# A conditioned transformer block on one core: where the transposed maxima's parts and their spreading stand among scores and values, and which queue carries the inverses

## The chip, the cores and the metric

The kernel runs on one core of a Trainium2 chip. The metric is device time in microseconds, the median of several runs. One further execution was taken with the hardware profiler; all spans, waits and clocks below are from that execution.

## What is computed

One block on x of shape (4, 1024, 512), in float32 throughout: a conditioned RMS norm, attention with 16 heads of 32, a second conditioned RMS norm and a SwiGLU feed-forward of width 2048, with the residual added twice.

```
norm(x)  = g(t) * x * rsqrt(mean(x*x) + 1e-6) + b(t)
a        = x + softmax(q k^T / sqrt(32)) v @ Wo.T     # q, k, v from norm1(x)
block(x) = a + (silu(n @ gate.T) * (n @ hid.T)) @ out.T   # n = norm2(a)
result   = x + block(x)
```

## The kernel before

The tokens are cut into 8 blocks of 512. Scores stand transposed, keys on the partitions, so one unit of score work r covers 256 keys, 4 heads and 256 queries: a tile `raw` of 128 x 2048. Four such units (256 keys each, 1024 in all) make one j, that is one group of heads for 256 queries. The main loop runs over slots g; slot g computes the scores of unit g, and g % 4 (`kind`) says which quarter of its j it is. Work on other units lies in the same slot: adding the shift and the exponential to unit g - 5 (`r_x`), multiplying unit g - 6 by the values (`r_v`).

For each j the softmax needs the maximum over all keys, which lie on partitions and in the four units. `running_max` (L290, L293) folds units elementwise into `rmax`; `max_T` (L299) transposes it on TensorE into a tile `mt` that shares the score banks `sc`; `parts` (L305 to L310) reduces on VectorE and splits the negated maximum into three bfloat16 parts in `split`; `parts_T` transposes them on TensorE (`pt`, L315) and copies them on ScalarE to `mT` (L317); `spread` multiplies them by a selecting matrix on TensorE (`sp`, L325), which puts the shift of two heads on all partitions, and copies that on ScalarE to `shift` (L326); it is called for heads 0 and 1 and for heads 2 and 3. `shifted` (VectorE, L330) adds `shift` to `raw`, `exponential` (ScalarE, L335) follows, and `weighted` (TensorE, `av`, L345) multiplies by the values. `keep` (ScalarE, L285) copies the scores from their bank to `raw`; the score tile `sc` has one buffer, so the next scores (L278) wait for it.

The denominators: `accumulate` adds the exponentials by a DMA from GpSimd's queue (L359), `fold_sum` (L367) folds them on VectorE, `sums` (TensorE, L377) sums over the keys, `sums_out` (ScalarE, `total`, L382) copies. The sums then go through DRAM to be inverted in a compact form: `compact` (L146), `take` (L152), `invert` (VectorE, L157), `put` (L162), and `spread_inverse` (L168), which reads each row to 32 partitions in four DMAs, the tile `rec`. All these DMAs are issued from ScalarE's queue. `normalize` (VectorE, L402) uses `rec` in the kind-2 slot after. The second norm's inverse roots `inv` take the same way (`norm_root`, `norm_compact`, `take`, `invert`, `put`, `norm_spread`), with slots given by `after(g0 + ...)` (end of the slot) and `between(g0 + ...)` (towards its end), where g0 = 32 (n + 1) for block n; then follow `norm_scale` (VectorE, L179), `norm_mod` (ScalarE, L182) and `token_sums` (VectorE, L465 to L471).

From slot 60 on (`FS`) the feed-forward of block n runs beside the attention of later blocks: one of 16 hidden tiles p for two slots, even and odd. It is computed with seven products of half size (a Strassen-like form): in the even slot `pair_26` (`pa`), `copy_156` (ScalarE, L516, to `pb`) and the contraction of an earlier tile (`filler`, `pc`, taken by VectorE in L554); in the odd slot `pair_7` (`pb`), `sub_5` (VectorE, L523), `pair_3` (`pa`), `gate_tanh` (ScalarE, L533), `pair_15` of the next tile (`pa`), `take_5` (ScalarE, L497), `gate` (VectorE, L538), `add_15` (VectorE, L501), `pair_4` (`pb`, which needs `sub_5`) and `hidden` (VectorE, L541). Before slot 60 the projections of keys, queries and values stand there instead (`chain`, with an `evict` in the slot or, for `late`, at the head of the next one).

Two banks of PSUM (tag `w` of pool `ps`) are shared by `pa`, `pc`, `pt`, `sp`, `sum`, `pm` (the norm's mean) and the projections: while `pa` holds one, the chain pc, pt, sp, sp, next pa goes through the other, each waiting until an engine has emptied it.

The order of instructions on TensorE, VectorE, ScalarE and GpSimd is the order of the calls in the code (a manual schedule). SyncE's queue, which carries the weights (`fw`: L477, L478, L480, L481; `ow`: L545; `wo`: L410), the loads of `kq` (L257, L258), `v` (L264) and `res` (L406), and the stores of keys and values (`st`, `sv`: L236, L249), is ordered by the scheduler. DMAs from SyncE and ScalarE share eight completion semaphores in turn, so that a DMA also waits until the previous one on its semaphore has landed.

Of the kernel before, what the change touches and what calls it, by code (L numbers as in the profile page):

```python
# [24 lines left out]
def tile_cond_transformer_block(  # L25
# [138 lines left out]
    def spread_inverse(tag: str, t, rows: int, n: int):  # L164

        src = inv_s.pop(tag).rearrange("(h p) c -> h (p c)", p=rows)
        for h in range(P // rows):
            nc.scalar.dma_start(  # L168
                out=t[h * rows : (h + 1) * rows, :], in_=src[h : h + 1, :].to_broadcast([rows, n])
            )  # L170

# [6 lines left out]
    def norm_scale(dst, tag: str, c: int):  # L178
        nc.vector.tensor_tensor(dst[:, c, :], dst[:, c, :], state[tag], ALU.mult)  # L179

    def norm_mod(which: int, b: int, dst, c: int):
        nc.scalar.activation(  # L182
            dst[:, c, :],
            dst[:, c, :],
            AF.Identity,
            bias=mod[:, (2 * which + 1) * C + c, b : b + 1],
            scale=mod[:, 2 * which * C + c, b : b + 1],
        )
# [136 lines left out]
            nc.tensor.matmul(pp[:, i, :], select[:, k + i, :], mT[j], start=True, stop=True)  # L325
        nc.scalar.copy(shift[j][:, k : k + 2, :], pp)  # L326

    def shifted(r: int):
        t = raw[r]
        nc.vector.tensor_tensor(  # L330
            t, t, shift[r // UN].unsqueeze(1).to_broadcast([P, 2, HG, HQ]), ALU.add
        )

    def exponential(r: int):
        nc.scalar.activation(raw[r], raw[r], AF.Exp)  # L335
# [182 lines left out]
    def pair_7(p: int):  # L518
        product(bank_b[p][:, RIGHT], fw[p, 1][:, 0], tokens(p // NF)[1])
# [52 lines left out]
    def between(g, fn, *a):  # L572
        halfway.setdefault(g, []).append((fn, a))

    def after(g, fn, *a):
        ended.setdefault(g, []).append((fn, a))
# [41 lines left out]
    for n in range(NBLK):  # L618
        g0 = (n + 1) * BS
        pin(g0 + 6, load_res, n)  # L620
        go = g0 + (14 if n < NBLK - 1 else 8)
        for d in range(C):
            first.append((go, None, project_out, (n, d)))
            pin(go - 3 + (d // 2 * 4 if n else 0), load_wo, n, d)
        if n < NBLK - 1:
            tag = f"f{n}"
            after(g0 + 18, add_res, n)
            for k in range(2):
                after(g0 + 17, lambda n=n, tag=tag, k=k: norm_squares(x2[n], tag, k))
            after(g0 + 18, norm_root, tag)  # L630
            after(g0 + 18, norm_compact, tag)
            after(g0 + 19, take, tag)
            between(g0 + 21, invert, tag)
            after(g0 + 21, put, tag)
            between(g0 + 23, norm_spread, tag)
            for c in range(C):
                after(g0 + 24, lambda n=n, tag=tag, c=c: norm_scale(x2[n], tag, c))
            for c in range(C):
                between(g0 + 25, lambda n=n, c=c: norm_mod(1, n // QB, x2[n], c))
            for i in range(3):  # L640
                after(g0 + 26, token_sums, n, i)
            between(g0 + 27, token_sums, n, 3)
# [23 lines left out]
    with tc.manual_schedule(  # L666
# [61 lines left out]
        while g < END:  # L728
            kind = g % UN
            r_x, r_v = g - UN - 1, g - UN - 2  # L730
            x_on, v_on = 0 <= r_x < NR, 0 <= r_v < NR
            j_m = g // UN - 1
            m_on = 0 <= j_m < NR // UN
            j_s = g // UN - 2
            s_on = 0 <= j_s < NR // UN
            j_n = g // UN - 3
            n_on = 0 <= j_n < NR // UN
            j_o = g // UN - 4
            o_on = 0 <= j_o < direct
            ffn = g >= FS  # L740
            p = (g - FS) // 2
            even = g % 2 == 0
            columns[0] = DH

            if kind == 1 and m_on:
                spread(j_m, 0)
            if g < NR:
                scores(g)
            if kind == 1 and m_on:
                spread(j_m, 2)  # L750
                mT.pop(j_m)
            if kind == 3 and s_on:
                fold_sum(j_s)
            if kind == 0 and n_on and j_n >= direct:
                inverse(j_n)
            if x_on:
                shifted(r_x)
            if late is not None:
                late()
                late = None  # L760
            if kind == 0 and n_on and j_n >= direct:
                normalize(j_n)
            if kind == 2 and o_on:
                normalize(j_o)
            if kind == 1 and n_on and j_n < direct:
                take(f"s{j_n}")
            if kind == 3 and n_on and j_n < direct:
                put(f"s{j_n}")
            for fn, a in pinned.pop(g, []):
                fn(*a)  # L770
            if g < NR:
                keep(g)
            if v_on:
                weighted(r_v)
                accumulate(r_v)
            if kind == 0 and o_on:
                sums_in(j_o)
            if kind == 1 and s_on:
                take_av(j_s)
            due = bool(first) and first[0][0] <= g  # L780
            if not ffn:
                if x_on:
                    exponential(r_x)
                credit = min(credit + PACE, 2.9)
                evict = None
                if credit >= 1 or due or kind == 0:
                    evict = chain(g, FG)
                    credit -= evict is not None
                if kind == 3 and s_on:
                    sums(j_s)  # L790
                    sums_out(j_s)
                if g < NR:
                    running_max(g, 0)
                    running_max(g, 1)
                if evict is not None:
                    evict()
                for fn, a in halfway.pop(g, []):
                    fn(*a)
                if kind == 0 and m_on:
                    columns[0] = P  # L800
                    max_T(j_m)
                    parts(j_m)
                if g == FS - 1:
                    columns[0] = DH
                    pair_15(0)
                    take_5(0)
                    add_15(0)
                elif credit >= 1 or due or kind == 0:
                    late = chain(g, FG)
                    credit -= late is not None  # L810
                if g in (FS - 4, FS - 3):
                    load_f(0, g - FS + 4)
                if g == FS - 1:
                    load_f(1, 0)
            elif even:
                load_f(p + 1, 1)
                pair_26(p)
                copy_156(p)
                if x_on:
                    exponential(r_x)  # L820
                if kind == 0 and m_on:
                    max_T(j_m)
                    parts(j_m)
                one, two, evict = filler(p)
                one()
                two()
                if g < NR:
                    running_max(g, 0)
                    running_max(g, 1)
                if evict is not None:  # L830
                    evict()
                for fn, a in halfway.pop(g, []):
                    fn(*a)
            else:
                load_f(p + 2, 0)
                if due or len(queue) > FG:
                    chain(g)()
                pair_7(p)
                sub_5(p)
                pair_3(p)  # L840
                gate_tanh(p)
                if x_on:
                    exponential(r_x)
                pair_15(p + 1)
                take_5(p + 1)
                if g < NR:
                    running_max(g, 0)
                gate(p)
                if g < NR:
                    running_max(g, 1)  # L850
                add_15(p + 1)
                pair_4(p)
                hidden(p)
                if due:
                    chain(g)()
                if kind == 3 and s_on:
                    sums(j_s)
                    if j_s < direct:
                        sums_out(j_s)
                for fn, a in halfway.pop(g, []):  # L860
                    fn(*a)
            if kind == 0 and m_on:
                parts_T(j_m)
            if kind == 2 and n_on and j_n < direct:
                invert(f"s{j_n}")
            columns[0] = DH
            for fn, a in ended.pop(g, []):
                fn(*a)
            if g == FS + 2 * FG - 2:
                load_ow(0)  # L870
            g += 1
# [91 lines left out]
```

## Time and profile before

| | |
|---|---|
| runs | 2629.59, 2631.21, 2634.0 us; median 2631.21 |
| profiled execution | 2638.34 us, span 2636.6 us |
| TensorE busy | 2419.9 us (92%), mean granted clock 0.977 |
| VectorE, ScalarE busy | 1819.3 us (69%), 1413.9 us (54%) |
| TensorE idle, 35 to 580 us (no feed-forward yet) | 545 - 483.1 = 61.9 us, clock 0.95 |
| TensorE idle, 580 to 2300 us (attention and feed-forward) | 1720 - 1591.2 = 128.8 us, clock 0.99 |
| TensorE idle, 2300 to 2637 us (feed-forward alone) | 337 - 320.2 = 16.8 us, clock 0.98 |
| four slots between 580 and 2300 us, undisturbed | 30.86 us |

Rows of the profile name the source line, the engine, and the tiles written and read; a bracket gives the idle time of the engine before the instruction and what ended it. `PEld` rows are weight loads. In a windows row the columns after the stretch and its length are the busy times of PE, PEld, DVE, ACT and POOL, each with its count, then the granted clock of TensorE, the busy share of the DMA engines and GB/s. Rows of waits give the waiting engine, tile and line, what it waited for, the time in all, how often, and the longest.

### The profile page before, as it was taken

To read this page: it belongs to the slowest core of one execution; us is meant where nothing else is said; L and a number is where in the kernel's file an instruction comes from. 1 tells how busy PE (TensorE), PEld (TensorE's weight loads), DVE (VectorE), ACT (ScalarE), POOL (GpSimd) and SP (SyncE) were. 2 spreads that over 40 slices of the span, in tenths; PEclk is the share of its full clock that TensorE was granted. 3 is DMA by queue.
4 is the path that set the end of the run, shared out by engine and by line. 5 is a ranking of instruction groups with operands and counts; after the bars stand their busy time and mean duration, and the time that the engine had idled before them with its cause. 6 is when DMAs were issued, how large, how long until landed. Compare 5 with 4: busy or idle time off the path is not lost. (4 is left out here: it accounts for less than half of the span.)

```text
span 2636.6 us, 71583 instructions
## 1 busy us (share of the span) xinstructions
PE 2419.9 (92%) x31785; PEld 1154.9 (44%) x31785; DVE 1819.3 (69%) x2116; ACT 1413.9 (54%) x1485; POOL 172.9 (7%) x207
## 2 busy tenths in 40 slices
PE   8988898888999999998999899998999999989999
PEld 3333333334444444444444454444444444434444
DVE  2667676767777877687868787887688777843332
ACT  3666566666555655565656565655566556522110
POOL 0000000000000000000000000000000000000000
PEclk9999989999999999999999999999999999999999
DMA  5698788887887888788878887888888888863442
GB/s 191 176 266 215 216 217 212 226 210 187 205 198 190 209 210 203 169 208 211 206 186 206 217 197 180 206 217 201 188 200 215 205 189 195 189 163 107 139 131 89
DMA packets 216386, 510.64 MB, mean 194 GB/s; under 512 B 43407, under 2 KB 84359, under 8 KB 188686
## 3 DMA queue, kind: packets, MB, share of 16 engines
q0 software_dynamic: 28656, 208.68, 41.7%
q1 hardware_dynamic: 153840, 286.59, 32.6%
q10 hardware_dynamic: 33582, 10.80, 1.9%
q8 instruction: 250, 4.10, 0.6%
q14 instruction: 58, 0.48, 0.1%
HBM read 254.82 MB, written 42.48 MB: 113 GB/s over the span
## 5 line engine op out<-in xcount | busy, mean ns | idle before, releaser
L330 DVE TENSOR_TENSOR raw<-raw,shift 128x2048 f32<-128x2048 f32 x256 | 585.1, 2286 | 196.2 <-ACT shift L326 196.2
L285 ACT COPY raw<-sc 128x2048 f32<-128x2048 f32 x256 | 478.7, 1870 | 216.9 <-PE sc L278 166.6
L335 ACT ACTIVATE raw<-raw 128x2048 f32<-128x2048 f32 x256 | 489.9, 1913 | 58.8 <-DVE raw L330 38.1
L290 DVE TENSOR_TENSOR rmax<-rmax,raw 128x1024 f32<-128x1024 f32 x384 | 469.0, 1221 | 59.8 <-ACT raw L285 56.5
L106 PE MATMUL pc<-h,ow 128*32 128x512 f32 x4096 | 467.7, 593 | 0.2 <-DVE rec L392 0.2
L106 PE MATMUL pa<-x,fw 128*32 128x256 f32 x6144 | 381.2, 381 | 8.2 <-DVE pa L501 4.9
L278 PE MATMUL sc<-kq 32*128 32x256 f32 x4096 | 308.2, 408 | 8.3 <-ACT raw L285 8.2
L359 POOL DMA_DIRECT2D raw<-raw x192 | 165.7, 863 | 2063.1 <-ACT raw L335 1000.9
L345 PE MATMUL av<-raw,v 128*32 128x256 f32 x4096 | 286.2, 398 | 11.3 <-ACT raw L335 11.2
L106 PE MATMUL pa<-sums,fw 128*32 128x256 f32 x4096 | 269.1, 380 | 0.0
L106 PEld LDWEIGHTS pa<-x,fw 128*32 128x32 f32 x6144 | 200.0, 111 | 155.2 <-issue 12.6
L106 PE MATMUL pkq<-y,wkq 128*32 128x512 f32 (+1 forms) x1760 | 241.7, 616 | 21.0 <-ACT total L382 11.7
L278 PEld LDWEIGHTS sc<-kq 32*128 32x128 f32 x4096 | 197.8, 189 | 133.4 <-issue 65.1
L106 PEld LDWEIGHTS pc<-h,ow 128*32 128x32 f32 x4096 | 128.0, 110 | 243.5 <-issue 217.3
L516 ACT COPY pb<-pa 128x256 f32<-128x256 f32 x128 | 46.0, 360 | 295.2 <-PE pa L106 133.9
L533 ACT ACTIVATE t<-pa 128x512 f32<-128x512 f32 x128 | 76.5, 598 | 188.8 <-PE pa L106 184.2
L106 PEld LDWEIGHTS pa<-sums,fw 128*32 128x32 f32 x4096 | 133.4, 110 | 88.7 <-issue 1.0
L345 PEld LDWEIGHTS av<-raw,v 128*32 128x32 f32 x4096 | 109.6, 111 | 141.0 <-issue 71.5
L554 DVE SCALAR_TENSOR_TENSOR res<-pc,res 128x512 f32<-128x512 f32 x128 | 88.5, 692 | 93.2 <-PE pc L106 92.8
L106 PE MATMUL pb<-sums,fw 128*32 128x256 f32 x2048 | 134.9, 381 | 12.0 <-DVE pb L523 12.0
L293 DVE TENSOR_TENSOR rmax<-raw 128x1024 f32<-128x1024 f32 x64 | 78.1, 1220 | 96.3 <-PE mt L299 54.5
L106 PEld LDWEIGHTS pkq<-y,wkq 128*32 128x32 f32 (+1 forms) x1760 | 73.3, 118 | 156.3 <-issue 128.5
(100 smaller groups left out, 1996.8 us busy)
## 6 DMA issues: line engine op xcount, KB each, us to landing
raw<-raw POOLq DMA_DIRECT2D x192, 1024.0 KB, 8.8
fw<-sw SPq DMA_DIRECT2D x256, 256.0 KB
ow<-in_out_w SPq DMA_DIRECT2D x128, 256.0 KB
fw<-in_gh_w SPq DMA_DIRECT2D x128, 256.0 KB
wkq<-in_kq_w SPq DMA_DIRECT2D x32, 512.0 KB
v<-vs SPq DMA_DIRECT2D x32, 512.0 KB
fw<-in_gh_w SPq DMA_DIRECT2D x128, 128.0 KB
kq<-kqs SPq DMA_DIRECT2D x31, 512.0 KB
```

Of the source, the lines that this page charges most:

```text
L106: nc.tensor.matmul(dst[k : k + n, :], w[:, k : k + n], moving, start=start, stop=stop, skip_group_check=seeded)
L278: nc.tensor.matmul(sc[:, i, k, :], t[rows, kt * P : (kt + 1) * P], t[rows, q0 : q0 + HQ], start=True, stop=True)
L285: nc.scalar.copy(raw[r].rearrange("p k h q -> p h k q"), state.pop(("sc", r)))
L290: nc.vector.tensor_tensor(rmax[j], rmax[j], raw[r][:, k, :, :], ALU.max)
L293: nc.vector.tensor_tensor(rmax[j], raw[r][:, 0, :, :], raw[r][:, 1, :, :], ALU.max)
L330: nc.vector.tensor_tensor(t, t, shift[r // UN].unsqueeze(1).to_broadcast([P, 2, HG, HQ]), ALU.add)
L335: nc.scalar.activation(raw[r], raw[r], AF.Exp)
L345: nc.tensor.matmul(av[j][i * DH : (i + 1) * DH, :], v[m][:, kt, i * DH : (i + 1) * DH], raw[r][:, k, i, :], start=(kt == 0), stop=(kt == K ...
L359: nc.gpsimd.dma_start(out=acc[j].rearrange("p k h q -> p (k h q)"), in_=raw[r].rearrange("p k h q -> p (k h q)"), accum_op=ALU.add,)
L516: nc.scalar.copy(bank_b[p][:, RIGHT], bank_a[p][:, RIGHT])
L533: nc.scalar.activation(state["t", p], bank_a[p], AF.Tanh, scale=0.5)
L554: nc.vector.scalar_tensor_tensor(r, pp, 0.5, r, ALU.mult, ALU.add)
```

## The change

What moves:

- `parts_T` moves from the end of the kind-0 slot to the head of the kind-1 slot. The first `spread` moves from ahead of the scores to behind them, the second from behind the scores to behind `weighted`. `shifted` of that slot is done in two halves of two heads each, behind the second `spread`. `keep` moves behind `weighted` and the second `spread`.
- With the feed-forward, `pair_7` and `sub_5` of the tile whose even slot is of kind 0 move to the end of that slot; in the kind-1 slot `gate_tanh` moves behind `take_5` and `gate` behind `add_15`.
- Before the feed-forward, `sums` and `sums_out` of the kind-3 slot move behind the late chain.
- The norm's steps from `norm_root` to `norm_mod` move by about one slot; `token_sums` stays.
- `spread_inverse` issues its DMAs from SyncE's queue.

```
         for h in range(P // rows):
-            nc.scalar.dma_start(
+            nc.sync.dma_start(
...
-    def shifted(r: int):
-        t = raw[r]
-        nc.vector.tensor_tensor(
-            t, t, shift[r // UN].unsqueeze(1).to_broadcast([P, 2, HG, HQ]), ALU.add
-        )
+    def shifted(r: int, heads: slice = slice(0, HG)):
+        t = raw[r][:, :, heads, :]
+        s = shift[r // UN][:, heads, :]
+        nc.vector.tensor_tensor(t, t, s.unsqueeze(1).to_broadcast(list(t.shape)), ALU.add)
...
-            after(g0 + 18, norm_root, tag)
-            after(g0 + 18, norm_compact, tag)
-            after(g0 + 19, take, tag)
-            between(g0 + 21, invert, tag)
-            after(g0 + 21, put, tag)
-            between(g0 + 23, norm_spread, tag)
+            between(g0 + 19, norm_root, tag)
+            between(g0 + 19, norm_compact, tag)
+            after(g0 + 20, take, tag)
+            between(g0 + 22, invert, tag)
+            after(g0 + 22, put, tag)
+            between(g0 + 24, norm_spread, tag)
             for c in range(C):
-                after(g0 + 24, lambda n=n, tag=tag, c=c: norm_scale(x2[n], tag, c))
+                after(g0 + 25, lambda n=n, tag=tag, c=c: norm_scale(x2[n], tag, c))
             for c in range(C):
-                between(g0 + 25, lambda n=n, c=c: norm_mod(1, n // QB, x2[n], c))
+                between(g0 + 26, lambda n=n, c=c: norm_mod(1, n // QB, x2[n], c))
...
             if kind == 1 and m_on:
-                spread(j_m, 0)
+                parts_T(j_m)
             if g < NR:
                 scores(g)
             if kind == 1 and m_on:
-                spread(j_m, 2)
-                mT.pop(j_m)
+                spread(j_m, 0)
...
-            if x_on:
+            if x_on and kind != 1:
                 shifted(r_x)
...
-            if g < NR:
-                keep(g)
             if v_on:
                 weighted(r_v)
                 accumulate(r_v)
+            if kind == 1 and m_on:
+                spread(j_m, 2)
+                mT.pop(j_m)
+                shifted(r_x, slice(0, HG // 2))
+                shifted(r_x, slice(HG // 2, HG))
+            if g < NR:
+                keep(g)
...
-                if kind == 3 and s_on:
-                    sums(j_s)
-                    sums_out(j_s)
                 if g < NR:
                     running_max(g, 0)
                     running_max(g, 1)
...
                 elif credit >= 1 or due or kind == 0:
                     late = chain(g, FG)
                     credit -= late is not None
+                if kind == 3 and s_on:
+                    sums(j_s)
+                    sums_out(j_s)
...
                 if evict is not None:
                     evict()
+                if kind == 0:
+                    pair_7(p)
+                    sub_5(p)
...
-                pair_7(p)
-                sub_5(p)
+                if kind == 3:
+                    pair_7(p)
+                    sub_5(p)
                 pair_3(p)
-                gate_tanh(p)
+                if kind == 3:
+                    gate_tanh(p)
                 if x_on:
                     exponential(r_x)
                 pair_15(p + 1)
                 take_5(p + 1)
+                if kind == 1:
+                    gate_tanh(p)
                 if g < NR:
                     running_max(g, 0)
-                gate(p)
+                if kind == 3:
+                    gate(p)
                 if g < NR:
                     running_max(g, 1)
                 add_15(p + 1)
+                if kind == 1:
+                    gate(p)
...
-            if kind == 0 and m_on:
-                parts_T(j_m)
```

## The prediction

> **What bounds the kernel now.** I read the page's busy times first, then PE's own waits, then the timeline of one undisturbed period of four slots, then a disturbed one and the windows of both. A "period" is the four slots of one unit j; slot kinds are g % 4.
>
> ```profile
> PE 2419.9 (92%) x31785; PEld 1154.9 (44%) x31785; DVE 1819.3 (69%) x2116; ACT 1413.9 (54%) x1485; POOL 172.9 (7%) x207
> ```
>
> TensorE is the bound; what can be won is its 216.7 us of idle time (span 2636.6), and time lost to a lower clock. PE's waits say where the idle time is:
>
> ```profile
> PE sp L325 <- ACT mT L317: 56.5, 64, 6.3
> PE pt L315 <- DVE res L554: 39.0, 48, 0.8
> ...
> PE pt L315 <- DVE split L310: 11.9, 6, 2.3
> PE pkq L106 <- ACT total L382: 11.7, 5, 3.5
> PE pmf L106 <- DVE res L554: 11.4, 6, 1.9
> ```
>
> Half of all idle time stands at the two steps that the change moves, `pt` and `sp`. An undisturbed period:
>
> ```profile
> 1718.99 0.27 PE L315 MATMUL pt<-ident_bf,split 128*128 128x128 bf16 x2 [0.81 <-DVE res L554]
> 1719.30 0.36 ACT L317 COPY mT<-pt 12x256 bf16<-12x256 bf16 x1 [1.08 <-PE pt L315]
> 1719.71 0.27 PE L325 MATMUL sp<-mT,select 12*128 12x256 bf16 x1 [0.45 <-ACT mT L317]
> ...
> 1721.83 2.29 DVE L330 TENSOR_TENSOR raw<-raw,shift 128x2048 f32<-128x2048 f32 x1 [2.89 <-ACT shift L326]
> ...
> 1737.80 0.42 DVE L523 TENSOR_TENSOR pb<-pb,p 128x256 f32<-128x256 f32 x1
> ...
> 1739.07 1.05 PE L106 MATMUL pb<-sums,fw 128*32 128x256 f32 x16
> ```
>
> PE waits 0.81 us for the bank that `pc` held and 0.45 us for the copy of `mT`: 1.26 us a period, 52 times between 582 and 2300 us. The last two lines show a cover that matters later: `pair_4` starts 0.85 us after `sub_5` ended. A disturbed period, and its clock:
>
> ```profile
> 1508.85 0.36 ACT L516 COPY pb<-pa 128x256 f32<-128x256 f32 x1 [10.28 <-DMA fw<-in_gh_w]
> ...
> 1511.33 0.37 PE L325 MATMUL sp<-mT,select 12*128 12x256 bf16 x1 [6.29 <-ACT mT L317]
> ```
>
> ```profile
> 1482.00:1504.00 22.00, 21.95 (x316) 10.54 (x309) 19.53 (x24) 10.84 (x9) 1.73 (x2) 1.00 0.84 187
> ...
> 1511.00:1518.00 7.00, 6.67 (x68) 3.84 (x71) 2.73 (x3) 3.49 (x6) 0.86 (x1) 0.56 0.90 193
> 1719.00:1750.00 31.00, 29.74 (x440) 15.50 (x439) 25.49 (x29) 19.27 (x19) 2.17 (x3) 1.00 0.91 225
> ```
>
> ScalarE's queue stood from 1497.14 to 1508.76 in the four L168 issues of `rec`; by the waits in the built program one of them needs the 1 MB load of `res` to have landed. Everything on ScalarE behind it was late; PE idled 6.29 us and then ran 7 us at a granted clock of 0.56 (second last column but two) against 1.00.
>
> **The undisturbed period.** Before, from the end of `pc` to `pair_26` of the kind-2 slot: 0.81 + (1728.38 - 1718.99) = 10.20 us. After, `pair_7` (0.86 start to start) stands between `pc` and `pt`; L554 ends 0.75 us after `pc` (1718.18 to 1718.93), so that wait is covered. From `pt`'s start, by start-to-start differences of the same timeline: `pt` 0.27, `sc` 1.07, `sp` 0.31, `av` 0.89, `sp` 0.31, `pair_3` 0.86, `pair_15` 1.73, `pair_4` 0.86, turn 0.12, `sc` 1.07, `av` 0.89: 8.38. With `pair_7` 9.24, so 0.96 is won and not 1.26: the first `sp` ran beside `sc` (0.01 start to start) and now stands alone like the second (0.31).
>
> The covers, in us from `pt`'s start. `mT` is ready at 0.72, `sc` lasts to 1.34. First shift copy 1.75 to 2.34 (0.41 behind its `sp`, 0.59 long); `av` covers it until 2.54. Second copy 2.95 to 3.54; `pair_3` covers it until 3.71. Then ScalarE has `keep`, now queued behind both copies, to 5.4 (1.88), `avs` to 5.75, the exponential to 7.66 (the halves of `shifted`, about 1.2 each by the 128x1024 maximum's 1221 ns, end at 4.75), `take_5` to 8.02; `add_15` ends 8.46 and `pair_26` starts at 8.52 where PE would come at 8.38: 0.14 lost. The tanh, now behind `take_5`, ends at 8.65; with gate and hidden (0.6 each) the next `shifted` starts at 9.88 instead of 9.17. From there to the end of `sub_5` in kind 3 VectorE took 9.45 (1728.16 to 1738.22, less 0.61 of waiting): 19.33. PE comes to `pair_4` at 19.14 to 19.2: the cover of 0.85 is gone and 0.19 is lost. Net 0.63, times 52: 33 us. Bounds: all idle time gone, 66; and below nothing, -0.3 each (-16), if the second copy's thin cover fails. I take 33, from the nearest rows.
>
> **Inverses on SyncE's queue.** 255 L168 issues and their waits leave ScalarE. Five waits of `sp` for `mT` were 4.49, 5.60, 6.29, 5.26 and 3.95 us, 23.3 above the usual 0.45 each; the periods behind them were 2.96, 2.17, 2.82, 1.90 and 3.08 over the undisturbed 30.86, the low clock: 12.9. Gain 36; bounds 0 (another ScalarE DMA takes over the wait) and 36. On SyncE the four `rec` (median 0.69 us an issue) stand ahead of `fw`'s last piece and the next pair's `fw`. That one was issued at 1744.88 and is used by `pair_15` a period after 1737.3, so 23 us later: priced at nothing, hidden by that slack; without it a period could lose what ScalarE's stall cost. One rule speaks against the move. The Trainium skill ("DMA: Bandwidth & Descriptors", section "Issuing engines are not separate DMA queues") says that DMAs of all issuing engines share the same 16 DMA engines, and that issuing from several only saves issuing time, usually small; by that the move is worth 0 and the sum 36 less. The 11.6 us above are no issuing time but a wait in order, so the row decides.
>
> **The first 582 us.** In kind 3 `sum` now comes behind the late chain: seven waits of `pkq`, `pv`, `pa` for `total` (21.1 us) each shrink by up to a chain's 3.43: 18. Four chains behind them took 5.2 to 5.6 instead of 3.6: 7. `sp` 13 x 0.45: 6. I take off 8, since `rec` now stands among the stores of `st`, for which ScalarE waited 36.5 us already: 23, bounds -15 and 40.
>
> **The norms, one slot later.** `norm_scale` (four at 685 ns) stood in VectorE's 2.89 us of idle time at kind 1's head; now it ends kind 1, inside the chain to `sub_5` that has no cover left. With 1.9 of `token_sums` and 0.7 of waiting for `norm_mod` (four at 813 ns, now just ahead of them), `sub_5` ends near 24.4 and `pair_4` waits 5.3 instead of 0.96 and, on `sum` behind it, 0.65: 3.7 six times is 22, and up to 2.5 of low clock each. I take -25, bounds 0 and -40. `norm_root` behind `sum`: six waits of 1.9 go (11), but its bank waits for `total` (0.8), `mt` for a `keep` behind the square root and its table (1.3), and in kind 1 two projections lose the cover of `av` for the second copy (0.75) and of an early gate (0.9): -8, bounds +8 and -20.
>
> **Sum.** 33 + 36 + 23 - 25 - 8 = 59. The profiled execution took 2638.3 us (span 2636.6), 7 above the runs' median of 2631.2: 2638.3 - 59 - 7 = 2572.
>
> **Rivals.** (a) Larger gain: the first `sp` still runs beside `sc`, and the norms fit. 66 + 36 + 35 - 5 = 132, so 2499. For it: both overlapped before. Against: VectorE is busy 25.49 of 31 us in that period. (b) Slower: VectorE's chain from tanh to `sub_5` bounds every period. With the queue's 36, norms at -45 and -8 and nothing in the first stage, it decides from 0.6 us of lateness at `pair_4` (52 x (0.96 - 0.63) = 17); at 1.5 us, 28 + 45 + 8 - 36 = 45 lost: 2676. For it: the used-up cover. Against: the sum above puts it at 0.2. (c) No change: ScalarE's other DMAs take over the wait, the first stage gives nothing, and the norms eat the period's gain: 33 - 33 = 0, 2631.
>
> **How the numbers follow.** Forecast 0.66, larger gain 0.20, slower 0.10, no change 0.04. The forecast's bounds, put together as roots of sums of squares, are 48 below and 74 above: 2524 to 2646. The range leaves out half of (a) and most of what lies in (b): 2505 to 2622. Within 0.2% (5 us, about what a measurement of this kernel can tell from no change) 0.04; faster 0.86; slower 0.10.
>
> **What would show it.** Right: `pt` no longer waits for `res`; `sp` waits for `mT` under 0.1 us; an undisturbed period of about 30.2 us; no `rec` on ScalarE's queue and no clock of 0.56 behind `res`'s load; a new wait of `pb` for `sub_5`, small in each period and near 5 us six times. Wrong: `pa` waiting for `shift` or `add_15` by over 0.5 us, PE waiting for `fw`, or `sc` for `keep`, in each period.

## The result, and the profile after

Five runs of the changed kernel took 2605.53 to 2618.26 us, median 2607.55; the kernel before, run between them, 2634.0. The ratio is 0.9914, 95% interval 0.9887 to 0.994: faster by 0.9%. The forecast was 2572. The direction was right and the size was not: 26.5 us won where 59 were summed. The profiled execution took 2606.2 us (span 2604.4), 32 less than the one before.

I cut both spans at two marks, the 14th and the last copy of `mT` on ScalarE: the stage before the feed-forward, the attention beside the feed-forward, the rest.

| us | to the 14th `mT` | to the last `mT` | rest |
|---|---|---|---|
| before | 581.9 | 1717.8 | 336.9 |
| after | 566.5 | 1705.7 | 332.1 |
| won | 15.3 | 12.1 | 4.8 |
| forecast | 23 | 33 + 36 - 25 - 8 = 36 | not priced |

The greater part of the miss, 24 us, is in the middle. The windows of that stretch, before and after:

```profile
581.88:2299.72 1717.84, 1589.35 (x22605) 799.43 (x22605) 1335.91 (x1541) 1012.74 (x1024) 134.56 (x156) 0.99 0.83 199
566.54:2272.27 1705.73, 1608.23 (x22605) 782.75 (x22605) 1359.76 (x1592) 1010.20 (x1025) 133.33 (x155) 0.99 0.83 201
```

TensorE's idle time there fell by 31.0 us (from 128.5 to 97.5), but its busy time grew by 18.9. In an undisturbed period 0.34 us of busy time are new (29.60 to 29.94), about what the prediction had for the first `sp`, which now stands alone; the periods of the norm grow by more. The busy times and TensorE's waits of the changed kernel (engine, tile, line, what it waited for; us in all, times, longest):

```profile
PE 2434.4 (93%) x31785; PEld 1134.6 (44%) x31785; DVE 1845.1 (71%) x2180; ACT 1409.4 (54%) x1485; POOL 172.4 (7%) x207
```

```profile
PE pb L106 <- DVE pb L522: 30.4, 10, 4.8
PE sum L376 <- DVE h L537: 23.0, 38, 0.7
PE av L344 <- ACT raw L334: 18.6, 17, 2.4
...
PE mt L299 <- ACT raw L285: 10.5, 12, 4.0
...
PE sp L325 <- ACT mT L317: 6.9, 4, 2.6
```

The two waits that the change aimed at are gone: `pt` for `res` (39.0) is no longer listed, `sp` for `mT` fell from 56.5 to 6.9. In their place stands a row that the prediction had only in the periods of the norm: `sum` waits for `h`, that is for `gate` (L537), 38 times (12 times and 5.9 us before). Rows from the timeline of an undisturbed period show it:

```profile
1811.19 0.42 DVE L522 TENSOR_TENSOR pb<-pb,p 128x256 f32<-128x256 f32 x1
1811.76 1.05 PE L106 MATMUL pb<-sums,fw 128*32 128x256 f32 x16
1812.65 0.68 DVE L537 SCALAR_TENSOR_TENSOR h<-t,pa 128x512 f32<-128x512 f32 x1
1813.39 0.64 PE L376 MATMUL sum<-raw,ones_sum 128*32 128x256 f32 x8 [0.58 <-DVE h L537]
...
1823.22 0.12 PEld L315 LDWEIGHTS <-split 128*128 128x128 bf16 x2 [0.41 <-DVE res L553]
1823.24 0.27 PE L315 MATMUL pt<-ident_bf,split 128*128 128x128 bf16 x2
1823.44 1.15 PE L278 MATMUL sc<-kq 32*128 32x256 f32 x16
1824.41 0.38 PE L325 MATMUL sp<-mT,select 12*128 12x256 bf16 x2
```

The matmuls of `pt` and `sp` carry no bracket: TensorE no longer idles ahead of them (only the weight load of `pt` still waits for `res`, beside `pair_7`). `pair_4` (1811.76) comes after `sub_5` (ends 1811.61) and does not wait either. But `sum` takes the bank that `gate` empties, and `gate` stands on VectorE behind `sub_5` and one maximum; TensorE came 0.58 us too early. The period is 30.52 us (1823.55 - 1793.03, two copies of `mT`), 0.34 less than before, not 0.63.

Rows from a disturbed period behind the load of `res` (issued at 1748.54), and the granted clock of its stretches (third last column):

```profile
1774.60 1.22 DVE L366 TENSOR_TENSOR raw<-raw 128x1024 f32<-128x1024 f32 x1 [2.44 <-DMA raw<-raw]
1774.68 1.87 ACT L285 COPY raw<-sc 128x2048 f32<-128x2048 f32 x1 [4.01 <-DMA raw<-raw]
1778.42 1.31 PE L106 MATMUL pb<-sums,fw 128*32 128x256 f32 x16 [2.30 <-DVE pb L522]
```

```profile
1757.00:1778.00 21.00, 19.12 (x294) 9.86 (x292) 16.07 (x17) 12.54 (x13) 1.72 (x2) 1.00 0.88 235
1778.00:1785.00 7.00, 6.16 (x60) 2.75 (x64) 6.36 (x8) 4.23 (x4) 0.86 (x1) 0.58 0.82 244
```

`rec` is off ScalarE's queue, and yet ScalarE stands: `keep` waits 4.01 us, now for the accumulating DMA (raw from raw, 1 MB, on GpSimd's queue), which must have read a tile before its buffer takes new scores. VectorE's `fold_sum` (L366) waits 2.44 us for a transfer of the same kind, and `shifted` and `sub_5` stand behind it; by this way TensorE idles 2.30 us further on. It then runs 7 us at a clock of 0.58, as it did at 0.56 before. These waits of `keep` were 14.4 us (12 times) before and are 46.6 (23 times) after:

```profile
ACT raw L285 <- DMA raw<-raw: 14.4, 12, 2.5
```

```profile
ACT raw L285 <- DMA raw<-raw: 46.6, 23, 5.4
```

### The profile page after: what moved, and what is told of

Read it like the earlier page. It is cut to its first block, busy times and chain, and to the rows that moved or that the text cites. A ratio compares the mean times of both kernels' runs of the same rounds, so it can differ in the third digit from the quotient of the medians.

```text
span 2604.4 us, 71655 instructions
## 1 busy us (share of the span) xinstructions
PE 2434.4 (93%) x31785; PEld 1134.6 (44%) x31785; DVE 1845.1 (71%) x2180; ACT 1409.4 (54%) x1485; POOL 172.4 (7%) x207
## 3 DMA queue, kind: packets, MB, share of 16 engines
q0 software_dynamic: 28656, 208.68, 41.5%
q1 hardware_dynamic: 166752, 296.56, 34.8%
## 5 line engine op out<-in xcount | busy, mean ns | idle before, releaser
L331 DVE TENSOR_TENSOR raw<-raw,shift 128x2048 f32<-128x2048 f32 (+1 forms) x320 | 595.1, 1860 | 128.6 <-ACT shift L326 123.3
L278 PE MATMUL sc<-kq 32*128 32x256 f32 x4096 | 302.3, 410 | 10.1 <-ACT raw L285 10.1
L344 PE MATMUL av<-raw,v 128*32 128x256 f32 x4096 | 282.2, 394 | 18.7 <-ACT raw L334 18.6
L106 PEld LDWEIGHTS pa<-x,fw 128*32 128x32 f32 x6144 | 194.6, 110 | 159.2 <-issue 24.6
L278 PEld LDWEIGHTS sc<-kq 32*128 32x128 f32 x4096 | 190.1, 189 | 145.8 <-issue 103.4
L305 DVE TENSOR_REDUCE top<-mt 128x8 f32<-128x1024 f32 x64 | 78.3, 1223 | 104.8 <-PE mt L299 104.8
L106 PE MATMUL pb<-x,fw 128*32 128x256 f32 x2048 | 134.0, 379 | 1.2 <-ACT pb L515 1.2
```

The lines of the kernel that those rows point to most:

```text
L106: nc.tensor.matmul(dst[k : k + n, :], w[:, k : k + n], moving, start=start, stop=stop, skip_group_check=seeded)
L278: nc.tensor.matmul(sc[:, i, k, :], t[rows, kt * P : (kt + 1) * P], t[rows, q0 : q0 + HQ], start=True, stop=True)
L305: nc.vector.tensor_reduce(top, state.pop(("mt", j)), AX.X, ALU.max)
L331: nc.vector.tensor_tensor(t, t, s.unsqueeze(1).to_broadcast(list(t.shape)), ALU.add)
L344: nc.tensor.matmul(av[j][i * DH : (i + 1) * DH, :], v[m][:, kt, i * DH : (i + 1) * DH], raw[r][:, k, i, :], start=(kt == 0), stop=(kt == K ...
```

## The experiments

Times are medians, ratios are to the kernel before run in the same call. "First" and "beside" are the first two stretches of the table above. Differences of under 5 us between kernels are not read.

| kernel | us | ratio, 95% | first | beside |
|---|---|---|---|---|
| the change | 2607.55 | 0.9914 (0.9887 to 0.994) | 566.5 | 1705.7 |
| 1 the change, inverses on ScalarE's queue | 2621.77 | 0.9942 (0.9923 to 0.9961) | 565.7 | 1721.5 |
| 2 before, inverses on SyncE's queue | 2603.55 | 0.9891 (0.9869 to 0.9913) | 580.9 | 1686.3 |
| 3 the change, norms in old slots | 2618.76 | 0.9931 (0.9911 to 0.9951) | 567.5 | 1716.4 |
| 4 the change, gate of kind 3 first | 2594.74 | 0.9847 (0.9828 to 0.9865) | 566.0 | 1696.5 |
| 5 as 2, sums behind the late chain | 2592.03 | 0.9848 (0.9824 to 0.9871) | 570.7 | 1682.1 |
| 6 as 5, parts moved before slot 60 | 2584.88 | 0.9818 (0.9796 to 0.984) | 566.2 | 1685.0 |
| 7 as 2, norms one slot later | 2622.15 | 0.9962 (0.9948 to 0.9977) | 575.9 | 1706.3 |
| 8 as 6, norms one slot later | 2604.74 | 0.989 (0.987 to 0.991) | 566.0 | 1702.5 |
| 9 as 6, pair_7 and sub_5 moved | 2575.55 | 0.9779 (0.9752 to 0.9807) | 566.0 | 1678.9 |
| 10 as 9, gate of kind 3 first | 2567.43 | 0.9752 (0.9725 to 0.9779) | 567.9 | 1675.3 |
| 11 as 6, parts moved everywhere | 2588.31 | 0.9832 (0.9805 to 0.9859) | 566.1 | 1687.0 |
| 12 as 3, gate of kind 3 first | 2614.33 | 0.9931 (0.9905 to 0.9957) | 567.5 | 1713.1 |
| 13 the change, tanh and gate of kind 1 old | 2591.24 | 0.9828 (0.9806 to 0.985) | 565.7 | 1690.7 |
| 14 as 10, parts moved everywhere | 2582.57 | 0.9793 (0.9767 to 0.982) | 568.2 | 1683.9 |
| 15 as 10, kq loads one slot earlier | 2566.78 | 0.9733 (0.971 to 0.9756) | 568.5 | 1671.1 |
| 16 the change, half accumulated | 2543.2 | 0.965 (0.9632 to 0.9669) | 537.2 | 1680.2 |
| 17 before, half accumulated | 2553.02 | 0.9686 (0.9666 to 0.9706) | 552.1 | 1668.6 |
| 18 as 12, half accumulated | 2512.37 | 0.9538 (0.9518 to 0.9557) | 536.7 | 1641.2 |

**1 and 2: the queue.** In `spread_inverse`, undone in the change and done alone in the kernel before:

```
-            nc.sync.dma_start(      # 1; in 2 the other way round
+            nc.scalar.dma_start(
```

> The changed kernel with the inverses' DMAs (L168) back on ScalarE's queue. Theory: the queue is worth about 20 us of the gain, since ScalarE then stands behind the 1 MB load of res five times again; 2627 us (2620 to 2634), waits of 4 to 6 us for something of ScalarE behind each load of res. Rival, the queue is worth nothing and the whole gain is the moved steps: 2607 us, no change from the changed kernel. By the prediction's own term (36 us): 2643.

> The kernel before with L168 on SyncE's queue and nothing else. Theory: 20 us faster than before, 2614; sp's five long waits for mT gone, the undisturbed period unchanged at 30.86 us. Rival, the queue is worth nothing: 2634. By the prediction's term: 2598.

Alone it wins 32 us, near the prediction's 36 and above the 20 that I expected by now, and more than the whole change. In the period of 1482 to 1518 that the prediction took apart, the copy of `mT` follows the last one after 30.87 us in place of 36.72; 30.6 of the 31.5 us won beside the feed-forward lie in the ten periods with and behind the last five loads of `res` there. TensorE's waits in kernel 2:

```profile
PE pt L315 <- DVE res L554: 39.0, 48, 0.8
PE sp L325 <- ACT mT L317: 31.2, 64, 2.9
```

The five long waits of `sp` (25.6 us) are gone, the small ones of every period stay. Inside the change the same line is worth only 14 us (2621.8 to 2607.6; kernel 1 lies within the 2620 to 2634 expected). So the parts do not add, and everything else in the change together wins 14 without the queue's move and nothing (4 us more) with it.

**3: the norms.** The steps from `norm_root` to `norm_mod` as in the kernel before:

```
-            between(g0 + 19, norm_root, tag)
+            after(g0 + 18, norm_root, tag)
...
-                between(g0 + 26, lambda n=n, c=c: norm_mod(1, n // QB, x2[n], c))
+                between(g0 + 25, lambda n=n, c=c: norm_mod(1, n // QB, x2[n], c))
```

> The changed kernel with the second norm's steps in the slots of before. Theory: the six periods of 36 to 37 us with norm_scale go back to about 33, so some 24 us: 2583 (2576 to 2592); pb's waits of 3.3 us for sub_5 gone. Rival 1, VectorE has no room in the old slots either, now that periods are shorter: 2600 or more. Rival 2, the DMA engines (busy 0.83) set the pace and give every saving back: less than 8 us, 2600 or more, with longer waits of keep for the accumulating DMA.

Missed: 11 us slower in place of 25 faster. The norms' own periods fall as expected (from between 36.1 and 37.1 us to between 33.1 and 34.7), but the period after the projection `po` rises from 30.6 us to between 31 and 37, with `keep` waiting for the accumulating DMA up to 6.0 us; these waits come to 69.0.

**4: gate of kind 3 first.**

```
+                if kind == 3:
+                    gate(p)
                 if g < NR:
                     running_max(g, 0)
-                if kind == 3:
-                    gate(p)
```

> The changed kernel with gate ahead of the first running_max in kind-3 slots, so that the bank that sum takes comes free one maximum (1.2 us) earlier. Theory: the wait of sum for gate (0.58 us, in every undisturbed period) goes, the period falls from 30.52 to 29.85 us, 50 times: 2574 (2568 to 2584). Rival 1, another wait takes its place (pair_26 for add_15, mt for keep): period 30.3 or more, 2597 or more. Rival 2, DMA sets the pace: period shorter but given back behind res, 2595 or more.

The new wait of `sum` for `gate` disappears and clean periods take 29.73, which shows that VectorE's order held `sum` up. The time fell by 13 us and not 33, as the second rival had it: at the same time `keep`'s waits for the accumulating DMA rose from 46.6 to 76.1.

**5 to 8: one part after the other.** Kernel 5 adds to kernel 2 the change's later `sums`, 6 to 5 the moved parts, `shifted` and `keep`, but only where

```
+            early = kind == 1 and m_on and g < FS
+            if early:
+                parts_T(j_m)
```

and 7 and 8 add the change's later norms to 2 and to 6.

> The kernel before with the inverses on SyncE's queue and, before slot 60, the sums behind the late chain; every other step in its old place. If the sums' place alone gives the first stage's gain (15 us after the whole change, of which at most 13 x 0.45 = 6 belong to the moved parts), the stage up to the 14th copy of mT shortens from 581 by 9 to 15 us and the time is 2589 to 2595. Rival: the sums' place gives nothing without the moved parts; 2603, like the queue alone.

> The same, and the parts' transposes and their spreading moved as in the change, but only before slot 60; with the feed-forward the old order, norms in their old slots. If what the change gains in the first stage and the queue's 32 us simply add, 2590 (2603.5 - 14); it would then beat the whole change by 17 us and show that the moved steps beside the feed-forward, with the norms, cost some 17. Rival: the queue and the first stage share their gain, 2600 or more.

> The kernel before with the inverses on SyncE's queue and the norms one slot later; all else old. If the later slot itself costs what the norm's periods grew by (3.3 to 4.2 us six times, 23), 2626. Rival: the later slot costs only behind the moved steps, where VectorE's chain to sub_5 has no cover left; in the old order it is free: 2603 to 2607.

> The whole change except the moves beside the feed-forward (pt, sp, shifted, keep, pair_7, sub_5, tanh and gate stay in their old places from slot 60 on). If those moves give what the undisturbed period shows (0.34 x 52 = 18), this kernel takes 18 us more than the whole change: 2625. Rival: behind the queue's move they cost more elsewhere than they gain in the undisturbed period, and leaving them out is faster: 2595 to 2605.

These do add: queue 32, sums 11.5, parts before slot 60 another 7, later norms minus 18.6 and minus 19.9. Kernel 8 is the whole change but for its moves beside the feed-forward, and takes 2604.7 against 2607.6: those moves, forecast at 33 us won, are worth nothing, and the rival's 2595 to 2605 held. Kernel 7 refutes the rival that the later norms cost only behind the moved steps.

**9 to 12: the moves beside the feed-forward, singly.**

```
+                if kind == 0:            # 9, at the end of the even slot
+                    pair_7(p)
+                    sub_5(p)
...
-                pair_7(p)
-                sub_5(p)
+                if kind == 3:
+                    pair_7(p)
+                    sub_5(p)
```

> The queue, the sums and the first stage as in the change; beside the feed-forward only pair_7 and sub_5 of the kind-0 tile moved to the end of their slot, ahead of pt; pt, sp, shifted, keep, tanh and gate in their old places, norms in their old slots. The wait of pt for res (0.81 x 48 = 39 us) goes. Theory: TensorE reaches sum 0.8 earlier, VectorE's gate of kind 3 only 0.4 (sub_5 leaves its chain), so sum waits about 0.4 and an undisturbed period is 30.4 to 30.5: 2585 - 52 x 0.4 = 2564. Rival: as in the whole change, waits of keep and mt for the accumulating DMA (raw for raw) come with the shorter period and eat it: 2580 to 2590.

> The same, with gate of kind 3 ahead of its running_max. If gate's place behind running_max is all that holds sum, the undisturbed period falls to 30.05 and the time to 2585 - 52 x 0.8 = 2543. Rival: the accumulating DMA takes over: undisturbed periods of 30.05, but waits of keep, mt and av for it in the others, 2560 to 2575.

> The queue, the sums and the first stage as in the change; beside the feed-forward pt, sp, shifted (in halves) and keep moved as in the change, but pair_7, sub_5, tanh and gate in their old places, norms in their old slots. Theory: sp's wait for mT goes (0.45) and the first sp stands alone (0.31), while shifted ends later by about 0.8 and with it gate and sum: the period is 0 to 0.7 longer, 2585 to 2620. Rival: the moved parts are harmless and the cost beside the feed-forward (34 us from this first-stage kernel to the change with its norms back) lies in pair_7, tanh and gate: 2575 to 2585.

Kernel 10 has the edit of kernel 4 on top, kernel 12 joins 3 and 4, and 11 is

```
-            early = kind == 1 and m_on and g < FS
+            early = kind == 1 and m_on
```

> The whole change with the norms back in their old slots and gate of kind 3 ahead of its running_max. If the two edits add (+11 and -13), 2606. Rival: the norms' old slots cost only because VectorE was late at sum; with the gate first the norms' 19 us (what their later slot costs in the old order) come back: 2576.

In 9 and 10 a clean period falls from 30.86 to 30.00 and 29.90, more than in the change, though fewer steps are moved; `sum` comes without a wait, `sp` keeps its 0.45. Rows from kernel 10:

```profile
1991.87 0.69 DVE L537 SCALAR_TENSOR_TENSOR h<-t,pa 128x512 f32<-128x512 f32 x1
1992.71 1.05 PE L106 MATMUL pb<-sums,fw 128*32 128x256 f32 x16
1993.58 0.61 PE L376 MATMUL sum<-raw,ones_sum 128*32 128x256 f32 x8
```

For kernel 9 my theory had `sum` wait 0.4 for `gate`; it did not, and 9 us were won, not 21: the rival was nearer, and `keep`'s waits rose from 33.9 (kernel 6) to 63.1. Kernel 10 lies in its rival's 2560 to 2575. The moved parts alone (11) cost nothing that can be read (3 us). Kernel 12 followed neither number. Its clean periods are as short as any (29.73), its time is one of the longest:

```profile
1924.03 0.86 POOL L358 DMA_DIRECT2D raw<-raw  x1 [13.03 <-ACT raw L334]
1937.18 0.86 POOL L358 DMA_DIRECT2D raw<-raw  x1 [12.29 <-DMA raw<-raw]
```

```profile
1936.73 1.86 ACT L285 COPY raw<-sc 128x2048 f32<-128x2048 f32 x1 [6.03 <-DMA raw<-raw]
```

One accumulating DMA, issued at 1924.03, was still under way 12 us later; the next one of its sum waited for it, and so did `keep`, 6.03 us.

**13 and 14: tanh and gate of kind 1.** In both, `gate_tanh` stands ahead of the exponential and `gate` ahead of `add_15` in kind 1 too.

```
-                if kind == 3:
-                    gate_tanh(p)
+                gate_tanh(p)
                 if x_on:
                     exponential(r_x)
                 pair_15(p + 1)
                 take_5(p + 1)
-                if kind == 1:
-                    gate_tanh(p)
```

> The whole change with tanh and gate of kind 1 back in their old places (tanh ahead of the exponential, gate between the two maxima). If the later tanh and gate are what the moves beside the feed-forward lose (2618.8 against 2585 - 9 + 3 = 2579 with the norms in their old slots), this is 20 to 35 us faster than the change: 2573 to 2588. Rival: they cost nothing by themselves, the loss lies in pair_7 and the moved parts together: 2600 to 2610.

> The kernel with pair_7 and sub_5 moved and gate of kind 3 first, and pt, sp, shifted and keep moved as in the change as well; tanh and gate of kind 1 old, norms old. It differs from the change with norms back and gate first (2614) only in tanh and gate of kind 1. Theory (late tanh and gate): 2567 + 3 = 2570. Rival (pair_7 and the moved parts together): 2600 to 2614.

13 is 16 us faster than the change; 14 is 32 us faster than 12, its counterpart. So the later tanh and gate cost 16 to 32 us; both times lie between theory and rival, so that a part of the loss lies elsewhere. In kernel 13 clean periods too are shorter than the change's (30.24 against 30.52). In 12 they are shorter than in 14 (29.73 against 30.15), and the cost lies in the disturbed periods: the period after `po` is 32 to 37 us in kernel 12 and 32 to 35 in 14, and `keep`'s waits for the accumulating DMA are 93.2 against 64.7:

```profile
ACT raw L285 <- DMA raw<-raw: 64.7, 24, 5.1
```

No run halves this DMA in kernel 14, so how much of the 32 us runs through it stays open.

**15: less traffic beside it.**

```
-        pin(m * MS - 2, load_kq, m)
+        pin(m * MS - (3 if m * MS > FS + 3 else 2), load_kq, m)
```

> The kernel with pair_7 and sub_5 moved and gate of kind 3 first, and the loads of keys and queries (768 KB) one slot earlier beside the feed-forward, so that they no longer start in the slot of res's load or beside the norm's inverse. If keep's waits for the accumulating DMA (59 us on ScalarE, 23 of them) come from these loads beside it, they fall below 30 and TensorE's wait of mt for keep (31.9) below 10: 2567 - 22 = 2545. Rival: the accumulating DMA takes 8.8 us at the median whatever runs beside it, and nine raw tiles are too few for the shorter period: the waits stay, 2562 to 2572.

The rival held: waits of `keep` 52.5 after 59.2, the time the same as kernel 10's. One load's place is not the cause.

**16 to 18: half the bytes.** These three kernels leave half of the terms out of three units in four of each sum, so only their times say anything.

```
-                out=acc[j].rearrange("p k h q -> p (k h q)"),
-                in_=raw[r].rearrange("p k h q -> p (k h q)"),
+                out=acc[j][:, 0, :, :].rearrange("p h q -> p (h q)"),
+                in_=raw[r][:, 0, :, :].rearrange("p h q -> p (h q)"),
```

> The whole change with the accumulating DMA carrying only the first half of the keys of a unit (512 KB in place of 1 MB); the sums then lack the other half of three units in four. Theory: keep's waits for it (47 us on ScalarE) go, and of the change's time 20 to 30 us: 2580 to 2588. Rival: these waits lie beside other work, VectorE's order sets the period: 2600 to 2608.

> The kernel before with the same half left out of the accumulating DMA. Its waits for it were 14 us, and the stall of ScalarE's queue behind res's load stays: 2620 to 2632 by the theory, so that the change would gain about 45 in place of 27. Rival: the DMA engines' load in general is what matters, and this kernel gains as much as the changed one: 2605 to 2615.

> The change with norms back and gate of kind 3 first, and the same half left out. If the 32 us by which this kernel lies behind the one with the early tanh and gate of kind 1 (2582.6) run through the accumulating DMA (waits of 93 against 65 us), it falls to 2560 to 2575. Rival: the late tanh and gate hold TensorE up by themselves: 2595 to 2612.

The change fell by 64 us and kernel 12 by 102, more than expected; the kernel before fell by 82, where my theory had at most 15, so its rival held and more. Clean periods stay what they were (30.52, 29.73 and 30.86); about 30 us of each gain lie in the first stretch, and beside the feed-forward the gains are 25.5, 71.9 and 49.2. ScalarE's waits for the DMA are 46.6 us in the change; kernel 17 has no such row, and in kernel 12, and in the change and kernel 12 with half the bytes, they are:

```profile
ACT raw L285 <- DMA raw<-raw: 93.2, 32, 6.0
```

```profile
ACT raw L285 <- DMA raw<-raw: 4.3, 2, 3.1
```

```profile
ACT raw L285 <- DMA raw<-raw: 19.3, 7, 3.2
```

In the kernel before, half the bytes also took away the stall that the queue's move was made against. The issues of `rec` on ScalarE's queue in two successive periods, the first 2.5 us behind the load of `res` (issued at 1441.05; at the same place the full kernel's took 11.62 us, at 1497.14):

```profile
1443.51 4.18 ACTq L168 DMA_DIRECT2D rec<-invss  x4
...
1474.10 3.35 ACTq L168 DMA_DIRECT2D rec<-invss  x4
```

No wait of `sp` for `mT` is over 0.8 us in this kernel.

With `keep`'s waits for the DMA nearly gone and no stall of the queue on either side, the order shows what it is worth by itself. Beside the feed-forward the change then takes 1680.2 against 1668.6, so it loses 11.5 us. By the copies of `mT`, periods of the same place compared: the six norm periods lose 24.7 in all; 22 clean ones win 0.34 each, 7.6; the six with a `po` and no norm win 1.04 each, 6; the six after the second `po` win some 5; the six with both lose 3; the first four lose 2.

What still stands open: whether the accumulating DMA's length comes from its own kind of transfer or from the 16 DMA engines' load in general; the half took away both. And the halved kernels do not show that this DMA is why the change fell short of its forecast, for beside the feed-forward the half is worth more in the kernel before (49.2 us) than in the change (25.5).

## Why the prediction was right or wrong

| step | forecast | by the runs |
|---|---|---|
| inverses' queue | 36 | 32 alone (kernel 2) |
| first 582 us | 23 | 18.7 in all (kernels 5 and 6), 14.7 of it in this stretch |
| norms later, with `norm_root` | -25 - 8 | -18.6, -19.9 (kernels 7 and 8) |
| undisturbed period | 33 | -3, not to be told from 0 (kernel 8 to the change) |
| sum | 59 | 28 (26.5 in the result's own runs) |

Added in this order, the queue and the first stretch came near their values, and the norms cost 19 us of the 33 that were priced. The failed one is **the undisturbed period**, 0.63 x 52 = 33; it stayed within its bounds (-16 to 66), but far from the value taken. That the sum missed by no more than 31 is in part luck: this term alone missed by 36, and the cheaper norms hid some of it.

The two profiles give a second account, by place. Of the 12.1 us won beside the feed-forward, the ten periods with and behind the last five loads of `res` win 24.0 (the queue, priced at 36), the six norm periods lose 23.4 (priced at 25), and all the others win 11.5, where 33 - 8 had been priced. By place, then, the undisturbed period (with the 8 for `norm_root`) and the queue each fell 12 to 14 us short.

The undisturbed period failed in three places.

The size per period was 0.34. From `pt` to `pair_26` TensorE took 8.35 us, and 9.39 before; the prediction had 8.38 and 0.14 of waiting for `add_15`, which did not come. On the other hand `pt` now starts 1.00 us after `pair_7` and not 0.86, right behind `res`; that the two cancel is luck. But from `pair_4` to `sum` 0.70 was lost (0.93 before, 1.63 after). What I left out was a waiter, though the norm's term had counted the same wait (0.65). I checked the cover of `pair_4` (by `sub_5`) and found it used up; `pair_4` held, with 0.15 to spare. But `sum`, the next on TensorE, takes a bank that `gate` of kind 3 empties, and that cover was zero in the profile before: `gate` ended at 1739.95, `sum` began at 1740.00. The rival (b) named VectorE's chain from tanh to `sub_5`; the chain was the right one and I ended it one instruction early. Kernel 4 shows it: with that gate ahead of the maximum the clean period is 29.73.

The count of 52 was wrong. There are 50 periods between the 14th and the last copy of `mT`, the row of `pt` that the prediction shows says 48, and in the profile before only 13 of the 50 are within 0.02 us of 30.86. With the DMA's load halved 23 win the 0.34 (one of them among the first four). The others hold a `po`, a norm or what comes after them, or are the first ones; they have their own limits, and move by -1.2 to +4.7 us.

And two moves that I had priced by VectorE's chain alone, the later tanh and gate of kind 1, cost 16 us in the change (kernel 13, whose clean period is 30.24). I had them end in 0.19 us at `pair_4`.

Added in another order the loss appears elsewhere: within the change the queue is worth 14 and not 36, and the norms' later slot wins 11 (kernel 3) in place of costing. What the rows show of the queue's part is what the prediction had only as rival (c), at 0.04: another DMA takes over ScalarE's wait. I looked for it among ScalarE's own DMAs; it was GpSimd's, through a tile's buffer (14.4 us before, 46.6 after). That this wait is the whole difference between 14 and 36 is not shown. Of the signs that I had listed as right, three failed: the period is 30.52 and not about 30.2, `pb` waits for `sub_5` 10 times and not in each period, and the clock behind `res`'s load still falls, to 0.58. None of the signs of being wrong came.

Of the smaller steps, the norm's period was priced by the right wait: `pb` waits 3.30 us for `sub_5` in the norm period, `av` 1.45 and `sum` 0.65, and with the DMA's load halved the six cost 24.7 against the forecast's 25. The cost of 8 for `norm_root` hardly showed: the periods after the second `po` fell, and the six with a `po` and a norm lose 3 with half the load. The rule of the Trainium skill that was weighed ("DMA: Bandwidth & Descriptors", section "Issuing engines are not separate DMA queues"), by which the move of the queue would be worth next to nothing, fails as a price here: kernel 2 changes nothing else and takes 32 us less, since what it takes off ScalarE is a wait in order. Its first half, that all queues share the same DMA engines, agrees with kernel 17, where half of GpSimd's bytes shortened the issues of `rec` on ScalarE's queue from 11.62 to 4.18 us.

Kernels 10 and 15 are the best full versions: ratio 0.9752 and 0.9733 against the change's 0.9914. They keep the queue, the sums and the first stage's parts, of the feed-forward's moves only `pair_7` and `sub_5`, add an earlier gate of kind 3, and leave the norms where they were.

## What to carry to other kernels

When TensorE is made to arrive earlier, list every instruction of the next stretch that waits for another engine, and its cover, not only the ones that the edit names; the first with none decides. Count the periods of each kind before multiplying by a gain, and ask what a shorter period leaves for the DMAs that must land within it. A change of several parts is best measured part by part: here the queue's move alone gave more (32 us) than all of them together (26.5).

## What was not expected of the hardware

The DMA that accumulates from one tile into another (199 of 1 MB, `add_res` among them) takes more of the DMA engines' time than its bytes suggest. In the changed kernel's queues (packets, MB, share of the 16 engines' span) it runs on the first:

```profile
q0 software_dynamic: 28656, 208.68, 41.5%
q1 hardware_dynamic: 166752, 296.56, 34.8%
```

208.68 MB took a larger share of the DMA engines' time than 296.56 MB on the second. A median issue of `accumulate` took 8.8 us to land, before as after, 5.6 with half the bytes, and up to 14.0. In these three kernels, halving it was worth 64 to 102 us, as much as the best order of instructions tried here (68, kernel 15) or more, though of all TensorE's waits in the changed kernel only one, of 2.6 us, is put down to a DMA.
